# 192 channels held as 128 and twice 64, and delta rows twice: a change of layout in two linear stages of a vision kernel

## The chip, the cores and the metric

One Trainium2 chip, of which the program uses one core. The metric is device time in microseconds (us). The kernel before takes 18009.72 us, the median of 3 runs (18006.15 to 18019.03). Engines are named as in the profile: PE (TensorE, matmuls; PEld its weight loads), DVE (VectorE), ACT (ScalarE), POOL (GpSimd), SP (which issues the DMAs).

## What is computed

Two layers, one after the other, on 8 images of 64 x 64 tokens with 192 channels, all in float32.

Layer 0 (cut to what matters):

```python
xz = einsum('bhwc,dc->bhwd', x, W_in)            # 192 -> 2 x 384
xl, z = split(xz, 2)
xc = silu(depthwise3x3(xl) + conv_b)
y0, y1 = state_space_scan(xc), state_space_scan(transpose(xc))   # two directions
yg = (y0 + y1) * silu(z)
out = x + einsum('bhwd,cd->bhwc', yg, W_out)     # 384 -> 192
h1 = silu(einsum('...c,dc->...d', out, W1) + b1) # 192 -> 768
x1 = out + einsum('...d,cd->...c', h1, W2) + b2  # 768 -> 192
```

Layer 1 takes one half of the channels of x1 through three convolutions, the other half through a second state-space model with four scan directions:

```python
x_dbl = einsum('bkdl,kcd->bkcl', xs4, x_proj_w)  # dts (6 rows), Bs, Cs (16 rows each)
delta = softplus(einsum('bkrl,kdr->bkdl', dts, dt_proj_w) + dt_proj_b)
h = exp(delta * A) * h + (delta * u) * B         # step by step over 4096 tokens
y = sum_n(h * C)
```

then a norm, a gate and a projection, and adds x1.

## The kernel before, in words

Channels lie on the 128 partitions, tokens along the free dimension. The program is written out by hand: every instruction is pinned to program order, so each engine runs its instructions in the order in which the Python code emits them, and waits for data by semaphores.

**The scan** (`selective_scan`) is the frame. It works through 3072 units: 8 images x 8 steps of 1024 tokens (`LC`) x 3 tiles of channels x 16 units. A unit is 8 channels x 16 states on 128 partitions, 1024 tokens. Per unit: SP fetches `dA` (`fetch`, four units ahead), ACT makes the exponential (`decay`, L1322), PE spreads `dB` (`spread`, L1330, two small bf16 matmuls), DVE multiplies (`weigh`, L1345) and scans (`scan`, L1352), POOL multiplies by C (L1356), ACT carries the end on (`carry_on`, L1362, L1363). Every four units PE sums the states (`gather`, L1374, four 32-column matmuls beside each other, into `acc`). `project` (L1227) makes the rows of dt, B and C for a step; `prepare` (L1257 on) makes delta for the next tile: two matmuls `ps_dt` (L1262, twelve rows of dt, one for each half of 512 tokens, in two half units), ACT operations on each, and then softplus on ACT and POOL.

**Side work.** All else of an image is written as Python generators, and class `Beside` deals their pieces out between the scan's instructions. While image b is scanned, the side work is `conv0`, `ssd` and `mlp0` (layer 0) of image b + 1, `conv_branch` with `scan_sums` and `scan_outputs` of image b - 1, and `scan_inputs` and `transposed` of image b + 1. Each piece ends with a `yield` of its cost, a number that stands for PE time. `selective_scan` calls `beside.half()` twice per unit. Each call adds a rate to a credit and runs pieces until the credit is used up; a `yield None` ends the half at once. The rate is

```python
self.rate = (own + sum(self.costs.get(gen.__name__, 40.0) for gen in self.stages)) / halves
```

with `own` = 465.0 for the scan's own PE work, which is taken from the same credit by `beside.spend`, and `halves` = 768 (720 for the first and the last image). `beside.finish()` runs what is left at the seam between two images: 23 units before the next image's first unit, just ahead of the next image's loads of `u` and of its side work. The first image's layer 0, `scan_inputs` and `transposed` have no scan to run beside: they are the prologue, the first 990 us.

**PSUM.** `cx.one(name)` hands out a bank of 128 x 512 float32. Beside the scan four such banks rotate among all that calls it (`acc`, `ps_dt`, and all side work); the scan's `dB` has the other four. In the prologue eight rotate.

**What the change touches.** `mlp0` (L649) works on 256 tokens at a time, 16 times per image, as stages in turn (`load, add, gate, turn, project, expand, contract, store`). The 192 channels are two times 96 (`CH`): each of gate (L693, `ps_z`) and expand (L739, `ps_h`) takes two matmuls with 96 rows per 128 outputs, added up in PSUM; project (L726, `ps_o`) and contract (L757, `ps_m`) make two outputs of 96 columns. `conv0`'s `rows_in` (L362, `ps_in`) does the same as gate, on 512 tokens. ACT takes the results out with Silu (L697, L744) or as a copy (L365). Silu and Exp are in different tables of ACT, so a Silu between two `decay` operations brings table loads (ACT_TABLE_LOAD).

Of the kernel before, what the change touches and what calls it, by code (L numbers as in the profile page):

```python
# [41 lines left out]
NXP = 4 * NS + 2 * RK  # L42
# [66 lines left out]
def setup(cx, cp, dp, p0, p1):  # L109
# [42 lines left out]
    k["b2"] = const(p0["b2"].rearrange("(a p) -> p a", p=CH), [CH, 2], "b2")  # L152
# [34 lines left out]
    nc.sync.dma_start(out=k["dtw"][4 * NS : NXP], in_=p1["dtw"].rearrange("g r t m -> r g t m"))  # L187
# [138 lines left out]

def conv0(cx, x):
# [3 lines left out]
    with cx.pool("cw0") as wp, cx.pool("v0", 2) as vp:  # L331
        w_in = wp.tile([CH, 2, INNER0], F32, tag="w_in", name="w_in")
        pin(nc.sync.dma_start(out=w_in, in_=k["p0_w_in"].rearrange("(a p) m -> p a m", p=CH)[:, :, :INNER0]))
# [11 lines left out]
        first = vp.tile([CH, 2, R2 * WW], F32, tag="xt", name="first")[:, :, :WW]  # L345
        pin(nc.sync.dma_start(out=first, in_=x[:, 0:WW].rearrange("(a p) l -> p a l", p=CH)))
        xts, xcs = {}, {}

        def load(p):

            n = min(R2, HH - 1 - p * R2)
            xts[p] = vp.tile([CH, 2, R2 * WW], F32, tag="xt", name="xt")
            at = (p * R2 + 1) * WW
            pin(nc.sync.dma_start(
                out=xts[p][:, :, : n * WW], in_=x[:, at : at + n * WW].rearrange("(a p) l -> p a l", p=CH)
            ))

        def rows_in(j, src, n, at):

            ps = cx.one("ps_in")  # L360
            for a in range(2):
                pin(nc.tensor.matmul(  # L362
                    ps[:, : n * WW], lhsT=w_in[:, a, j * 128 : (j + 1) * 128], rhs=src[:, a, :], start=a == 0, stop=a == 1
                ))
            pin(nc.scalar.copy(  # L365
                pads[j][:, at : at + n, 1 : 1 + WW], ps[:, : n * WW].rearrange("p (h w) -> p h w", w=WW)
            ))

        def project(p, j):
            pad = pads[j]  # L370
            if p == 0:
                rows_in(j, first, 1, 1)
            else:
                pin(nc.gpsimd.tensor_copy(pad[:, 0:2, :], pad[:, R2 : R2 + 2, :]))
            for b in range(2):
                n = min(RB, HH - 1 - p * R2 - b * RB)
                if n < RB:
                    pin(nc.gpsimd.memset(pad[:, R2 + 1, :], 0.0))
                rows_in(j, xts[p][:, :, b * RB * WW : (b * RB + n) * WW], n, 2 + b * RB)
                yield 2.4  # L380
# [268 lines left out]
def mlp0(cx, x, x1):  # L649

    nc, pin, k = cx.nc, cx.pin, cx.k
    NF, T = HID // 128, 256
    with cx.pool("mw0") as wp, cx.pool("m0", 2) as mp:
        def weight(n, shape, src):
            t = wp.tile(shape, F32, tag=n, name=n)
            pin(nc.sync.dma_start(out=t, in_=src))
            return t

        w_z = weight("w_z", [CH, 2, INNER0], k["p0_w_in"].rearrange("(a p) m -> p a m", p=CH)[:, :, INNER0:])
        w_out = weight("w_out", [128, NJ, C], k["p0_w_out"].rearrange("(j p) m -> p j m", p=128))  # L660
        w1 = weight("w1", [CH, 2, HID], k["p0_w1"].rearrange("(a p) m -> p a m", p=CH))
        w2 = weight("w2", [128, NF, C], k["p0_w2"].rearrange("(f p) m -> p f m", p=128))
        gT = wp.tile([128, NJ, T], F32, tag="gT", name="gT")
        h1 = wp.tile([128, NF, T], F32, tag="h1", name="h1")
        tiles = (slice(0, 2), slice(2, 3))
        st = {}

        def cols(i):
            return slice(i * T, (i + 1) * T)

        def load(i):
            st[i] = {}
# [934 lines left out]
```

## Time and profile before

| | |
|---|---|
| median of 3 runs | 18009.72 us |
| profiled execution | 17986.38 us |
| its span (first to last instruction) | 17984.4 us |
| mean granted clock of TensorE | 0.815 of full speed |
| busy: PE, DVE, ACT, POOL | 80%, 68%, 60%, 67% |
| scan of h, DVE L1352 | 3072 x 2343 ns |
| weigh, DVE L1345 | 3072 x 1218 ns |
| matmuls of mlp0, PE L693, L726, L739, L757 | 437.2, 395.9, 749.3, 750.1 us busy |
| `ps_in`, PE L362 | 398.6 us busy |
| `ps_dt`, PE L1262 | 558.4 us busy |
| ACT_TABLE_LOAD | 1283 ns each |

Busy time is the union of a group's records: two matmuls that run at once count once, so the sum of count x mean can be above it. A float32 matmul appears as two records (two passes). A waiting engine is listed with the instruction that released it.

### The profile page before, as it was taken

To read this page: it belongs to the slowest core of one execution; us is meant where nothing else is said; L and a number is where in the kernel's file an instruction comes from. 1 tells how busy PE (TensorE), PEld (TensorE's weight loads), DVE (VectorE), ACT (ScalarE), POOL (GpSimd) and SP (SyncE) were. 2 spreads that over 40 slices of the span, in tenths; PEclk is the share of its full clock that TensorE was granted. 3 is DMA by queue.
4 is the path that set the end of the run, shared out by engine and by line. 5 is a ranking of instruction groups with operands and counts; after the bars stand their busy time and mean duration, and the time that the engine had idled before them with its cause. 6 is when DMAs were issued, how large, how long until landed. Compare 5 with 4: busy or idle time off the path is not lost. (4 is left out here: it accounts for less than half of the span.)

```text
span 17984.4 us, 224777 instructions
## 1 busy us (share of the span) xinstructions
PE 14375.7 (80%) x76904; PEld 5676.6 (32%) x76904; DVE 12309.3 (68%) x9392; ACT 10711.9 (60%) x18482; POOL 12008.5 (67%) x6437
## 2 busy tenths in 40 slices
PE   8977788788877888778878788787888778868776
PEld 4623332343223431334313342233422334211111
DVE  2167787776667766677657775677766777667785
ACT  2464676466664756647566485664756557555654
POOL 3168776776668755687657875678755786657774
PEclk9987788789787887878878798787987779877676
DMA  3277777777677776777767777777776777677785
GB/s 85 75 201 177 189 190 202 168 193 199 170 195 174 192 194 164 196 176 201 186 170 188 176 199 185 184 188 178 197 183 178 184 183 198 180 194 190 184 196 143
DMA packets 1600969, 3238.93 MB, mean 180 GB/s; under 512 B 391580, under 2 KB 869396, under 8 KB 1596244
## 3 DMA queue, kind: packets, MB, share of 16 engines
q1 hardware_dynamic: 1599828, 3224.55, 71.2%
q8 instruction: 614, 10.06, 0.3%
q14 instruction: 527, 4.32, 0.1%
HBM read 2545.63 MB, written 678.18 MB: 179 GB/s over the span
## 5 line engine op out<-in xcount | busy, mean ns | idle before, releaser
L1356 POOL TENSOR_TENSOR h<-h,bc 128x1023 f32<-128x1023 f32 x3072 | 7223.5, 2354 | 3926.6 <-DVE h L1352 3412.2
L1352 DVE TENSOR_TENSOR_SCAN h<-dA,carry,dB 128x1024 f32<-128x1024 f32 x3072 | 7198.8, 2343 | 624.0 <-ACT dA L1322 188.7
L1345 DVE TENSOR_TENSOR dB<-dB,bc 128x1024 f32<-128x1024 f32 x3072 | 3741.5, 1218 | 2996.7 <-PE dB L1330 2948.1
L1322 ACT ACTIVATE dA<-dA,neg_a 128x1024 f32<-128x1024 f32 x3072 | 3486.8, 1135 | 797.5 <-DMA dA<-dld 795.3
L1374 PE MATMUL acc<-h,gather 128*32 128x512 f32 x12288 | 2479.9, 758 | 525.7 <-POOL h L1356 203.2
L1378 ACT COPY y<-acc 128x512 f32<-128x512 f32 x1536 | 886.5, 577 | 1908.7 <-PE acc L1374 1891.4
L1330 PE MATMUL dB<-dus,spread 24*128 24x512 bf16 x6144 | 1418.8, 430 | 365.3 <-DVE h L1352 283.8
L795 PE MATMUL ps_c<-p,conv_w 96*96 96x512 f32 x2304 | 1250.9, 670 | 120.5 <-ACT p L816 105.8
L1330 PEld LDWEIGHTS <-spread 24*128 24x128 bf16 x6144 | 317.6, 93 | 2607.9 <-issue 1700.3
L620 PE MATMUL ps_y<-dtx,M 64*64 64x64 f32 x12288 | 824.3, 267 | 393.5 <-DVE Hn L611 387.1
L1363 ACT ACTIVATE h<-h,bc 128x1 f32<-128x1 f32 x3072 | 905.1, 295 | 163.3 <-ACT carry L1362 3.8
L620 PEld LDWEIGHTS ps_y<-dtx,M 64*64 64x64 f32 x12288 | 691.6, 177 | 572.8 <-issue 349.5
L1374 PEld LDWEIGHTS acc<-h,gather 128*32 128x32 f32 x12288 | 321.2, 119 | 1690.8 <-issue 836.4
L319 PE MATMUL ps_cv<-pad,diag 64*64 64x512 f32 x6912 | 849.9, 611 | 5.6 <-ACT xo L399 2.8
L1276 POOL TENSOR_TENSOR w<-w,e 128x1024 f32<-128x1024 f32 x192 | 452.6, 2357 | 510.7 <-ACT carry L1362 423.7
L757 PE MATMUL ps_m<-h,w 128*96 128x256 f32 x3072 | 750.1, 392 | 30.2 <-DVE gT L715 20.4
L739 PE MATMUL ps_h<-o,w 96*128 96x256 f32 x3072 | 749.3, 397 | 4.3 <-ACT zs L697 1.7
L1362 ACT COPY carry<-h 128x1 f32<-128x1 f32 x3072 | 575.4, 187 | 250.9 <-DVE h L1352 248.1
L739 PEld LDWEIGHTS ps_h<-o,w 96*128 96x128 f32 x3072 | 585.6, 196 | 174.6 <-issue 62.3
L795 PEld LDWEIGHTS ps_c<-p,conv_w 96*96 96x96 f32 x2304 | 367.5, 177 | 814.8 <-issue 703.3
L555 PE MATMUL ps_d<-R,after 128*128 128x384 f32 x1024 | 554.8, 631 | 84.6 <-DVE M L575 36.8
L106 ACT ACT_TABLE_LOAD x481 | 617.1, 1283 | 8.2
(244 smaller groups left out, 22124.1 us busy)
## 6 DMA issues: line engine op xcount, KB each, us to landing
dA<-dld SPq DMA_DIRECT2D x3072, 512.0 KB
dud<-terms SPq DMA_DIRECT2D x192, 768.0 KB
dus<-dud SPq DMA_DIRECT2D x2304, 64.0 KB
bc<-bcd SPq DMA_DIRECT2D x256, 512.0 KB
X<-xrows SPq DMA_DIRECT2D x1024, 96.0 KB
yrows<-yo SPq DMA_DIRECT2D x1024, 96.0 KB
y<-yrows SPq DMA_DIRECT2D x256, 384.0 KB
u<-u SPq DMA_DIRECT2D x192, 512.0 KB
```

The costliest lines, as they stand in the source:

```text
L319: pin(nc.tensor.matmul(ps[64 * b : 64 * (b + 1)].rearrange("p (h w) -> p h w", w=WW), lhsT=diag[:, t, :], rhs=pad[64 * i : 64 * (i + 1), b ...
L620: pin(nc.tensor.matmul(psy[d][here, h * HP : (h + 1) * HP], lhsT=M[here, d, h, :], rhs=dtx[here, d, h, :], start=True, stop=d == 1,))
L739: pin(nc.tensor.matmul(ps[:, n * T : (n + 1) * T], lhsT=w1[:, a, (f + n) * 128 : (f + n + 1) * 128], rhs=o[:, a, :], start=a == 0, stop=a ...
L795: pin(nc.tensor.matmul(ps.rearrange("p (h w) -> p h w", w=WW), lhsT=w[:, t, :], rhs=pad[:, dy : dy + RB, dx : dx + WW], start=t == 0, stop ...
L1322: pin(nc.scalar.activation(dAs[q], dAs[q], AF.Exp, scale=k["neg_a"][:, steps[m][1], t, i : i + 1]))
L1330: pin(nc.tensor.matmul(dBs[q][:, half, :], lhsT=k["spread"][at : at + 3 * UD, :], rhs=du_of[n][at : at + 3 * UD, i // 2, :], start=True, s ...
L1345: pin(nc.vector.tensor_mul(dBs[q], dBs[q], of(q)[0]))
L1352: pin(nc.vector.tensor_tensor_scan(order(h, g), order(dA, g), order(dB, g), carry, ALU.mult, ALU.add))
L1356: pin(nc.gpsimd.tensor_mul(h[:, rest], h[:, rest], C_[:, rest]))
L1363: pin(nc.scalar.activation(end, end, AF.Identity, scale=C_[:, last : last + 1]))
L1374: pin(nc.tensor.matmul(ps[32 * v : 32 * (v + 1)], lhsT=k["gather"], rhs=hs[q - 3 + v][:, here], start=True, stop=True))
L1378: pin(nc.scalar.copy(y[:, here], ps))
```

## The change

- `mlp0` and `conv0` hold the 192 channels as a tile of 128 channels and a tile of 64 channels in which two blocks of tokens lie below each other (partitions 0 to 63 and 64 to 127). `load_split` loads weights so (the 64-row part twice), and `product` makes the result of two blocks: two matmuls with 128 rows, then two with 64 rows, one in each half of the rows of PE. Where 192 channels are the output, `narrow` makes 128 columns for both blocks in one matmul of 512 tokens, and then 64 columns for each block, one in each half of the columns of PE.
- `mlp0` thus takes 512 tokens at a time, 8 times per image, with an order of its own in place of `in_turn`: gate(i), expand(i-1), turn(i), contract(i-1), project(i). Silu(z) is written into `gT`, and `turn` multiplies there in place. The costs in its yields are new, and so are those in `conv0`.
- The rows of dt are made twice in `project` (rows 64 to 75 and 96 to 107, by doubled weight columns), so `prepare` issues the two `ps_dt` matmuls one behind the other on different rows of PE. Both banks are taken at once; the ACT operations on them stay in the half units in which they were. `own` becomes 450.0.

The diff, cut to its core (`load`, `first` and the setup of `b2` follow the same layout):

```diff
-NXP = 4 * NS + 2 * RK
+DTS = (64, 96)
+NXP = DTS[1] + 2 * RK
...
-    nc.sync.dma_start(out=k["dtw"][4 * NS : NXP], in_=p1["dtw"].rearrange("g r t m -> r g t m"))
+    for at in DTS:
+        nc.sync.dma_start(out=k["dtw"][at : at + 2 * RK], in_=p1["dtw"].rearrange("g r t m -> r g t m"))
...
+def load_split(cx, pool, tag, src, m):
+    a, b = (pool.tile([128, m], F32, tag=tag + v, name=tag + v) for v in "ab")
+    cx.pin(cx.nc.sync.dma_start(out=a, in_=src[0:128]))
+    for i in range(2):
+        cx.pin(cx.nc.sync.dma_start(out=b[64 * i : 64 * (i + 1)], in_=src[128:C]))
+    return a, b
+def product(cx, outs, weight, cols, xa, xbs):
+    nc, pin = cx.nc, cx.pin
+    for out, x in zip(outs, xa):
+        pin(nc.tensor.matmul(out, lhsT=weight[0][:, cols], rhs=x, start=True, stop=False))
+    for b, (out, x) in enumerate(zip(outs, xbs)):
+        pin(nc.tensor.matmul(out, lhsT=weight[1][64 * b : 64 * (b + 1), cols], rhs=x, start=False, stop=True))
...
-        w_in = wp.tile([CH, 2, INNER0], F32, tag="w_in", name="w_in")
-        pin(nc.sync.dma_start(out=w_in, in_=k["p0_w_in"].rearrange("(a p) m -> p a m", p=CH)[:, :, :INNER0]))
+        w_in = load_split(cx, wp, "w_in", k["p0_w_in"][:, :INNER0], INNER0)
...
         def project(p, j):
             pad = pads[j]
+            cols = slice(j * 128, (j + 1) * 128)
             if p == 0:
-                rows_in(j, first, 1, 1)
+                ps = cx.one("ps_in")
+                product(cx, [ps[:, :WW]], w_in, cols, [first[0]], [first[1]])
+                rows_in(j, ps, 1, 1)
             else:
                 pin(nc.gpsimd.tensor_copy(pad[:, 0:2, :], pad[:, R2 : R2 + 2, :]))
-            for b in range(2):
-                n = min(RB, HH - 1 - p * R2 - b * RB)
-                if n < RB:
-                    pin(nc.gpsimd.memset(pad[:, R2 + 1, :], 0.0))
-                rows_in(j, xts[p][:, :, b * RB * WW : (b * RB + n) * WW], n, 2 + b * RB)
-                yield 2.4
+            ns = blocks(p)
+            if ns[1] < RB:
+                pin(nc.gpsimd.memset(pad[:, R2 + 1, :], 0.0))
+            pss = [cx.one("ps_in") for b in range(2)]
+            xa, xb = xts[p]
+            product(
+                cx, [ps[:, : n * WW] for ps, n in zip(pss, ns)], w_in, cols,
+                [xa[:, b * RB * WW : (b * RB + n) * WW] for b, n in enumerate(ns)],
+                [xb[64 * b : 64 * (b + 1), : n * WW] for b, n in enumerate(ns)],
+            )
+            yield 1.8
+            for b, n in enumerate(ns):
+                rows_in(j, pss[b], n, 2 + b * RB)
+            yield 1.8
...
+        gT = wp.tile([128, 2, NJ, T], F32, tag="gT", name="gT")
+        h1 = wp.tile([128, NF, 2, T], F32, tag="h1", name="h1")
...
+        def load_x(i):
+            a = mp.tile([128, 2 * T], F32, tag="xa", name="xa")
+            pin(nc.sync.dma_start(out=a, in_=x[0:128, i * 2 * T : (i + 1) * 2 * T]))
+            b = mp.tile([128, T], F32, tag="xb", name="xb")
+            for v, low in enumerate(lows):
+                pin(nc.sync.dma_start(out=b[low], in_=x[128:C, (2 * i + v) * T : (2 * i + v + 1) * T]))
+            xs[i] = a, b
...
+        def gate(i):
+            for js in tiles:
+                pss = [cx.one("ps_z") for b in range(2)]
+                n = js.stop - js.start
+                for j in range(n):
+                    at = slice(j * T, (j + 1) * T)
+                    cols = slice((js.start + j) * 128, (js.start + j + 1) * 128)
+                    product(cx, [ps[:, at] for ps in pss], w_z, cols, *both(*xs[i]))
+                    if j + 1 < n:
+                        yield 1.8
+                for b, ps in enumerate(pss):
+                    pin(nc.scalar.activation(
+                        gT[:, b, js, :].rearrange("p j t -> p (j t)"), ps[:, : n * T], AF.Silu
+                    ))
+                yield 1.8
+            cx.exp_again()
+        def turn(i):
+            for b, (y, _) in enumerate(ys.pop(i)):
+                pss = []
+                for js in tiles:
+                    ps = cx.one("ps_t")
+                    for j in range(js.start, js.stop):
+                        for q in range(2):
+                            at = (j - js.start) * T + q * 128
+                            pin(nc.tensor.transpose(ps[:, at : at + 128], y[:, q, j * 128 : (j + 1) * 128], k["ident"]))
+                    pss.append(ps)
+                yield 1.2
+                yield None
+                for js, ps in zip(tiles, pss):
+                    g = gT[:, b, js, :].rearrange("p j t -> p (j t)")
+                    pin(nc.vector.tensor_mul(g, ps[:, : (js.stop - js.start) * T], g))
+        def narrow(weight, n, rhs, psa, psb):
+            for f in range(n):
+                pin(nc.tensor.matmul(psa, lhsT=weight[:, f, 0:128], rhs=rhs(f), start=f == 0, stop=f == n - 1))
+                yield 1.2
+            for f in range(n):
+                for b, low in enumerate(lows):
+                    pin(nc.tensor.matmul(
+                        psb[low, :T], lhsT=weight[:, f, 128:C], rhs=rhs(f)[:, b, :], start=f == 0, stop=f == n - 1
+                    ))
+                yield 0.6
+        def project(i):
+            xa, xb = xs.pop(i)
+            oa = mp.tile([128, 2 * T], F32, tag="oa", name="oa")
+            ob = mp.tile([128, T], F32, tag="ob", name="ob")
+            psa, psb = (cx.one("ps_o") for v in range(2))
+            yield from narrow(w_out, NJ, lambda j: gT[:, :, j, :], psa.rearrange("p (b t) -> p b t", b=2), psb)
+            yield None
+            pin(nc.vector.tensor_add(oa, psa, xa))
+            pin(nc.vector.tensor_add(ob, psb[:, :T], xb))
+            os[i] = oa, ob
+        def expand(i):
+            for f in range(0, NF, 2):
+                pss = [cx.one("ps_h") for b in range(2)]
+                for n in range(2):
+                    at = slice(n * T, (n + 1) * T)
+                    cols = slice((f + n) * 128, (f + n + 1) * 128)
+                    product(cx, [ps[:, at] for ps in pss], w1, cols, *both(*os[i]))
+                    if n == 0:
+                        yield 1.8
+                for n in range(2):
+                    for b, ps in enumerate(pss):
+                        pin(nc.scalar.activation(
+                            h1[:, f + n, b, :], ps[:, n * T : (n + 1) * T], AF.Silu, bias=k["b1"][:, f + n : f + n + 1]
...
+                yield 1.8
+        def contract(i):
+            oa, ob = os.pop(i)
+            psa, psb = (cx.one("ps_m") for v in range(2))
+            yield from narrow(w2, NF, lambda f: h1[:, f, :, :], psa.rearrange("p (b t) -> p b t", b=2), psb)
+            yield None
+            pin(nc.vector.scalar_tensor_tensor(oa, psa, k["b2"][:, 0:1], oa, ALU.add, ALU.add))
+            pin(nc.vector.scalar_tensor_tensor(ob, psb[:, :T], k["b2"][:, 1:2], ob, ALU.add, ALU.add))
+            yield 0.6
+            yield None
+            pin(nc.sync.dma_start(out=x1[0:128, i * 2 * T : (i + 1) * 2 * T], in_=oa))
+            for v, low in enumerate(lows):
+                pin(nc.sync.dma_start(out=x1[128:C, (2 * i + v) * T : (2 * i + v + 1) * T], in_=ob[low]))
+        load_x(0)
+        load_y(0)
+        for i in range(NI + 1):
+            if i < NI:
+                yield from gate(i)
+                add(i)
+            if i > 0:
+                yield from expand(i - 1)
+            if i < NI:
+                yield from turn(i)
+                if i + 1 < NI:
+                    load_x(i + 1)
+                    load_y(i + 1)
+            if i > 0:
+                yield from contract(i - 1)
+            if i < NI:
+                yield from project(i)
...
-            for i, here in enumerate(halves):
-                ps = cx.one("ps_dt")
-                pin(nc.tensor.matmul(
-                    ps, lhsT=k["dtw"][4 * NS : NXP, g, t, :], rhs=rows[4 * NS : NXP, here], start=True, stop=True
-                ))
-                beside.spend(1.2)
+            pss = [cx.one("ps_dt") for here in halves]
+            for ps, at, here in zip(pss, DTS, halves):
+                took = slice(at, at + 2 * RK)
+                pin(nc.tensor.matmul(ps, lhsT=k["dtw"][took, g, t, :], rhs=rows[took, here], start=True, stop=True))
+            beside.spend(1.2)
+            for i, (ps, here) in enumerate(zip(pss, halves)):
                 yield 1 + i
...
-        beside.spread_over(halves, 465.0)
+        beside.spread_over(halves, 450.0)
...
-                (4 * NS + RK * e, w[:RK]),
+                *((at + RK * e, w[:RK]) for at in DTS),
```

## The prediction

> **What bounds the kernel now.** I read the page first: busy times, then the chain that ended last.
>
> ```profile
> PE 14375.7 (80%) x76904; PEld 5676.6 (32%) x76904; DVE 12309.3 (68%) x9392; ACT 10711.9 (60%) x18482; POOL 12008.5 (67%) x6437
> ...
> PE 14%; DMA 10%; ACT 7%; POOL 6%; DVE 6%; issue 3%; SPq 1%; DVEq 0%; POOLq 0%; ACTq 0%
> ```
>
> No engine is full and the chain hops between all of them; PE (TensorE) has most in both. The view of waits says what the scan stands for:
>
> ```profile
> POOL h L1356 <- DVE h L1352: 3412.2, 1383, 24.4
> DVE dB L1345 <- PE dB L1330: 2948.1, 959, 111.3
> ```
>
> POOL only follows DVE. DVE needs 2.343 + 1.218 = 3.56 us per unit (3072 units), and its great wait is for `dB`, a small matmul queued on PE behind side work. So PE time counts where it holds `dB` up. Busy times by stretch: the prologue's MLP, then MLP, conv branch and scan_outputs beside the scan of image 3.
>
> ```profile
> core 0: us, PE busy (x) PEld busy (x) DVE busy (x) ACT busy (x) POOL busy (x), PEclk, DMA share, GB/s
> 524.00:790.00 266.00, 257.26 (x1215) 207.63 (x1214) 40.61 (x81) 129.52 (x187) 28.74 (x18) 0.98 0.21 64
> ...
> 8153.00:8675.00 522.00, 451.14 (x1920) 248.07 (x1924) 400.79 (x288) 412.38 (x656) 370.64 (x168) 0.89 0.76 195
> 8675.00:9005.00 330.00, 283.67 (x768) 77.96 (x760) 191.26 (x108) 153.67 (x279) 187.96 (x97) 0.89 0.73 192
> ```
>
> The prologue's MLP is PE alone. The MLP beside the scan takes 522 us for 104 units, 5.0 us each: PE 4.34, DVE 3.85, ACT 3.97 per unit. The last view is the timeline at the seam between two images (7178 on; the last line is the first seam):
>
> ```profile
> 7189.23 14.62 ACT L994 COPY part<-whole 128x1024 f32<-128x1024 f32 x8 [10.69 <-issue]
> ...
> 7220.95 1.09 PE L362 MATMUL ps_in<-first,w_in 96*128 96x64 f32 x4 [42.14 <-DMA y<-y]
> 7230.53 1.23 DVE L1345 TENSOR_TENSOR dB<-dB,bc 128x1024 f32<-128x1024 f32 x1 [48.95 <-PE dB L1330]
> ...
> 2834.37 1.23 DVE L1345 TENSOR_TENSOR dB<-dB,bc 128x1024 f32<-128x1024 f32 x1 [23.91 <-PE dB L1330]
> ```
>
> At 7180 the next image's side work is added, but what is left of this one's must be issued first, in one piece: some of `scan_inputs` and all of `transposed`. PE stands 42 us at the next conv0's first matmul, since SP issues that load only after `transposed`'s copies and stores. At the first seam `transposed` had been spread in time: 24 us.
>
> **What the skill says.** TensorEngine Tiling (Array Packing), Key Properties: a change of tiling mode drains TensorE. TensorE: Matmul & The Clock Gate, The mechanism (Part 3): matmuls on different row or column groups run together. The PE timeline agrees with both:
>
> ```profile
> 603.33 5.35 PE L757 MATMUL ps_m<-h,w 128*96 128x256 f32 x24
> 608.51 3.83 PE L739 MATMUL ps_h<-o,w 96*128 96x256 f32 x17
> ...
> 149.04 1.70 PE L408 MATMUL ps_p<-xp,xc 64*128 64x140 f32 x24
> 150.67 5.81 PE L319 MATMUL ps_cv<-pad,diag 64*64 64x512 f32 x52
> ...
> 7176.43 1.06 PE L1374 MATMUL acc<-h,gather 128*32 128x512 f32 x8
> 7177.43 0.39 PE L1330 MATMUL dB<-dus,spread 24*128 24x512 bf16 x2
> ```
>
> A matmul of f32 shows as two passes. 24 passes of 256 columns take 5.18 us: 0.216 each, 0.84 ns a column. The 24 half-height passes of 140 columns would take 2.83 one by one; they took 1.63: pairs (1.42) and a switch (0.2). `acc`'s eight passes, four at a time, are 2 x 0.43 = 0.86, and `dB`, in another mode, starts after 1.00: a switch of 0.14. I take 0.16. The same page's Part 1 has the clock fall when PE idles; here 0.98 in the prologue and 0.89 beside the scan. PSUM — Partial Sum Buffer, Specifications: 8 banks. Beside the scan four rotate in `one`, the others hold `dB`.
>
> **The change, part by part.** *MLP matmuls*, per 512 tokens. Before, 72 matmuls = 144 passes x 0.216 = 31.1 us. After, nine products of 4 full and 2 paired passes, and `narrow` with 3 and 6 steps of two long passes (4 short) and two paired ones: 54 + 18 + 36 = 108 pass times, 23.3 us; but each product enters and leaves the 64-row mode (18 switches), each `narrow` the 64-column mode (4): 22 x 0.16 = 3.5. Net 26.8, 4.3 saved, 34 us an image; gate and expand gain almost nothing (1.62 for 1.73 per product). *conv0*: twelve products of 512 columns: 3.46 - 2.59 - 0.32, 7 us an image. *dt*: the groups show 558.4 us busy for 384 matmuls, 1.45 each; two go as one, so 24 tiles x 1.45 = 35 us an image. The twelve rows sit in row groups of their own, in `dB`'s mode.
>
> *ACT*: Silus come in fours, not twos; in program order table loads fall from 1197 to 1000, 197 x 1.283 us / 8 = 32 us an image. DVE: the same counts, hidden. DMA: the same bytes; 16 more issues of some 0.5 us for x and x1 an image and 8 in conv0, hidden because `dA` is fetched four units ahead; without that cover 12 us. The store comes half a unit after its add, so `dA` fetches behind it on SP can wait; same cover. Wider `rows` copies cost nothing (partitions).
>
> *The spreading.* Each half unit gives side work rate = (own + costs)/768. Summing yields: mlp0 347.2 to 283.2, conv0 251.2 to 236.8, own 465 to 450, so 2.230 becomes 2.109. Stepping the credit through the yields, conv0, ssd, mlp0, branch, outputs, scan_inputs took 154, 183, 207, 108, 50, 66 halves with 13 of cost and `transposed` left over; now 151, 181, 179, 111, 51, 84, and `transposed` fills the last 11. So MLP loses 14 units, and the seam loses its bulk work.
>
> *MLP beside the scan.* PE after: 451 - 34/0.89 - 9 (dt) - 19 (14.5 units' own matmuls, 1.31 each) = 389 for 89.5 units, 4.34 as before. ACT: 412 - 32 - 36 = 344, 3.84. So 5.0 us a unit again. Against it stands a wait the trace doesn't show: banks now go in pairs, and the third pair waits for the first pair's four Silus. Bound: 0 (PE waits for ACT are 12 us in that window) to 1 us per pair, nine pairs per 512 tokens, 0.8 us a unit. I take 0.1: the copies have a product of 3 us to hide in. 89.5 x 5.1 = 456 for 520: -64 an image.
>
> *The rest of an image.* scan_inputs, `transposed` and seam: before 178 (33 units) + 65 (2) = 243. In image 0, which was spread so already, 51 units took 245, 4.80 each; 47.5 x 4.80 = 228, and a seam of 33 as the first: +18. Other stages: 31 us of PE saved there (dt 25, conv0 6), and I count 12, as waits of other kinds end there too. Sum -58. For images 1 to 5 -290, with 20 back for image 1, whose MLP took 500; image 6's seam was short (39): -32. Together -302. Image 0: MLP -60, `scan_inputs` with `transposed` +12, 9.5 units of scan alone at 4.4 +42, 2.5 more units of conv0 and ssd +9, dt -10: -7. Image 7: dt alone, -12. Prologue (eight banks, PE full): -34, conv0 -5. Sum -360: span 17984 to 17624; the median shown, 18009.7, is 25 above that execution's span: **17650**.
>
> **The rivals.** *Pair waits decide* (slower). Place: `product` in mlp0 beside the scan, four banks, the ACT queue ahead of the Silus. For it: at 8303 ACT stood 7.1 us for a late `dA` and PE then waited 3.5 for a bank with single ones already. Against: 12 us in 522. It turns the sign at 360/8 = 45 us an image, 0.6 us per pair; at 1 us, 8 x (72 - 45) slower: 18220. *Halves do not overlap*: the switches are added and nothing is saved, PE at 5.0 and the MLP at 5.7 us a unit: 54 us an image, dt's 12 and the prologue's 67 on top: 18200. `ps_p` speaks against. *DMA holds the MLP*: its bytes (102 MB) lose only 14.5 units' dA; 90 MB at 190 instead of 198 GB/s is 20 us an image: 17790. For it: 195 GB/s now; against: conv0's stretch runs at 205. *PE converts fully*: MLP at 4.8 a unit (-27) and the others at two thirds (-10), seven images: 17390.
>
> **How the numbers follow.** Likeliest 0.47 (its own range 17500 to 17830), full conversion 0.17, DMA 0.20, pair waits 0.10, no overlap 0.03, else 0.03. Time 17650; the range 17370 to 17920 leaves out the slower rival, no overlap and the fast end of full conversion. 0.2% (36 us) is about what a measurement of this kernel can tell from no change. Faster: 0.47 + 0.17 + 0.20 = 0.84; pair waits between 0.6 and 0.7 us leave 0.05 within; slower 0.11.
>
> **What would show it.** MLP stretches near 456 us; `ps_h`'s paired passes starting together; DVE's wait at the seams near 24 us, not 49; wait of PE for ACT in the MLP below 40 us an image; the prologue's MLP near 230 us; dt's PE time halved; 250 us less of ACT tables. The prediction is wrong if PE waits for Silus at every third pair, or if switches cost over 0.3 us.

## The result, and the profile after

The changed kernel takes 17895.4 us (median of 4 runs, 17849.8 to 17937.8), the kernel before 18014.4 us beside it (4 runs): a ratio of 0.9936 (95% interval 0.9914 to 0.9959). The sign was right and the time lies in the range, but only 119 us came where 360 were forecast. The profiled execution took 17849.8 us, span 17848.0.

From the page of the changed kernel, the busy times and the chain that ended last:

```profile
PE 13899.7 (78%) x75752; PEld 4872.4 (27%) x75752; DVE 12241.7 (69%) x9264; ACT 10450.0 (59%) x18285; POOL 12006.8 (67%) x6437
...
PE 13%; DMA 10%; ACT 8%; DVE 6%; POOL 5%; issue 4%; SPq 1%; DVEq 0%; POOLq 0%; ACTq 0%
```

PE has 476 us less to do, ACT 262 us less. The span fell by 136. The chain is as mixed as it was. The view of waits, the same two lines as before:

```profile
POOL h L1426 <- DVE h L1422: 3474.7, 1393, 22.4
DVE dB L1415 <- PE dB L1400: 3067.7, 879, 108.6
```

At this pace DVE waits longer for `dB` (3068 us, before 2948), although PE's work fell: PE comes later with less to do. The stretches, with the columns of the prediction's table: the prologue's MLP, then MLP and conv branch beside the scan of image 3.

```profile
500.00:737.00 237.00, 228.99 (x1078) 125.17 (x1079) 33.19 (x62) 92.52 (x160) 28.91 (x16) 0.97 0.27 84
...
8113.00:8582.00 469.00, 380.76 (x1684) 162.21 (x1685) 342.62 (x242) 353.15 (x579) 320.70 (x147) 0.87 0.75 194
8582.00:8923.00 341.00, 282.78 (x778) 77.58 (x777) 197.93 (x112) 156.34 (x283) 194.03 (x100) 0.91 0.74 193
```

Where PE is alone, the prologue, its gain arrives whole: 237 us for 266. Beside the scan the MLP takes 469 us for 89 units, 5.27 each, where it took 522 for 104, 5.0 each. PE's busy time per unit fell from 4.34 to 4.28, so more of each unit is PE standing, and the granted clock of the stretch is 0.87 for 0.89. The timeline (start, duration, instruction, idle time before it): a product of the MLP with `dB` behind it and the start of a later one, then the seam at 7157 and the first seam.

```profile
8310.53 1.13 PE L350 MATMUL ps_h<-oa,w1a 128*128 128x256 f32 x4
8311.59 0.70 PE L352 MATMUL ps_h<-ob,w1b 64*128 64x256 f32 x4
8312.23 0.39 PE L1400 MATMUL dB<-dus,spread 24*128 24x512 bf16 x2
...
8316.81 1.13 PE L350 MATMUL ps_h<-oa,w1a 128*128 128x256 f32 x4 [0.46 <-ACT h L807]
...
7171.32 0.66 PE L350 MATMUL ps_in<-first,w_ina 128*128 128x64 f32 x2 [17.98 <-DMA xa<-in_x_dram]
7182.65 1.23 DVE L1415 TENSOR_TENSOR dB<-dB,bc 128x1024 f32<-128x1024 f32 x1 [33.96 <-PE dB L1400]
...
2840.74 1.23 DVE L1415 TENSOR_TENSOR dB<-dB,bc 128x1024 f32<-128x1024 f32 x1 [23.45 <-PE dB L1400]
```

The paired passes do overlap: four of them end 0.70 us after they start, and the next matmul starts 0.64 us after they did, where four passes of 0.216 one by one would be 0.86. The seam is shorter: DVE waits 34 us where it waited 49, the first seam is as it was.

Where the 136 us of the two profiled executions came from, read off the scan's records from seam to seam: prologue -36, image 0 +44, image 1 +8, images 2 to 6 -35, -12, -4, -2 and -8, image 7 -90. (The border is the scan of the 23rd unit before the next image, so the seam ahead of image 7, shorter by some 29 us, is in its -90.) Images 1 to 6, where 302 us were expected, gave 53. Their stages, as means over images 2 to 6; a stage is taken here from its first matmul to the next stage's first, so its borders are a few us off those of the prediction, which followed the credit:

| | before, us | after, us |
|---|---|---|
| seam | 53 | 25 |
| conv0 | 373 | 378 |
| ssd | 571 | 565 |
| mlp0 | 509 (104 units, 4.89 each) | 460 (89 units, 5.17 each) |
| conv branch | 337 | 344 |
| scan_outputs | 164 | 164 |
| scan_inputs, transposed | 180 | 237 |
| sum | 2186 | 2174 |
| PE busy in it | 1767 | 1707 |

PE lost 60 us of work an image and the image 12 us. 48 us more of idle PE stand between them.

### The profile page after: what moved, and what is told of

Read it like the earlier page. It is cut to its first block, busy times and chain, and to the rows that moved or that the text cites. A ratio compares the mean times of both kernels' runs of the same rounds, so it can differ in the third digit from the quotient of the medians.

```text
span 17848.0 us, 222371 instructions
## 1 busy us (share of the span) xinstructions
PE 13899.7 (78%) x75752; PEld 4872.4 (27%) x75752; DVE 12241.7 (69%) x9264; ACT 10450.0 (59%) x18285; POOL 12006.8 (67%) x6437
## 5 line engine op out<-in xcount | busy, mean ns | idle before, releaser
L1400 PE MATMUL dB<-dus,spread 24*128 24x512 bf16 x6144 | 1368.2, 433 | 464.7 <-DVE h L1422 368.4
L661 PE MATMUL ps_y<-dtx,M 64*64 64x64 f32 x12288 | 750.9, 251 | 359.0 <-DVE Hn L652 355.7
L661 PEld LDWEIGHTS ps_y<-dtx,M 64*64 64x64 f32 x12288 | 630.3, 162 | 561.9 <-issue 357.2
L596 PE MATMUL ps_d<-R,after 128*128 128x384 f32 x1024 | 594.9, 672 | 95.2 <-DVE M L616 57.3
L350 PE MATMUL ps_h<-oa,w1a 128*128 128x256 f32 x1536 | 495.8, 449 | 160.7 <-ACT h L807 94.2
L598 ACT ACTIVATE M<-ps_d 128x384 f32<-128x384 f32 x512 | 247.2, 488 | 443.0 <-PE ps_d L597 442.5
L776 PE MATMUL ps_m<-h,w 128*128 128x512 f32 x768 | 417.2, 683 | 96.4 <-ACT h L807 54.5
L1297 PE MATMUL ps_xp<-u,xp 128*108 128x512 f32 x768 | 442.2, 663 | 57.2 <-DMA u<-u 36.6
```

The source lines that it names most:

```text
L661: pin(nc.tensor.matmul(psy[d][here, h * HP : (h + 1) * HP], lhsT=M[here, d, h, :], rhs=dtx[here, d, h, :], start=True, stop=d == 1,))
L1400: pin(nc.tensor.matmul(dBs[q][:, half, :], lhsT=k["spread"][at : at + 3 * UD, :], rhs=du_of[n][at : at + 3 * UD, i // 2, :], start=True, s ...
```

## The experiments

Ratios are to the kernel before on the same chip, where its median was 17986 to 17998 us. Where nothing else is said, all of a kernel computes what the changed one does.

### One part alone, or one part taken back

`dt_only`: the kernel before with dt's part.

```diff
-NXP = 4 * NS + 2 * RK
+DTS = (64, 96)
+NXP = DTS[1] + 2 * RK
...
+            pss = [cx.one("ps_dt") for here in halves]
+            for ps, at, here in zip(pss, DTS, halves):
...
-        beside.spread_over(halves, 465.0)
+        beside.spread_over(halves, 450.0)
...
-            po = vp.tile([128, 2, 2 * NP0], F32, tag="po", name="po")
+            po = vp.tile([128, 2, 2 * NP0], F32, tag="po", name="po", bufs=1)
```

> The kernel before with the dt part of the change alone (dt rows and weights twice, both halves of a row together, 450 for 465), MLP and input projection as before; conv0's tile po has one buffer instead of two, for room. The prediction counted 12 us an image for it, 8 x 12 = 96: 17918. If the last image's 90 us of the changed kernel are dt's alone (its MLP and conv0 are not beside that image), the same in all eight would be some 500: 17500. If PE's time for dt is hidden everywhere: within 36 us of 18014. Theory A of the lost gain (pair waits eat what MLP and conv0 save) needs a value near the changed kernel's 17895, between 17850 and 17950.

Measured: 17852.2 us, ratio 0.9918 (0.9895 to 0.9941). dt's part alone gives as much as the whole change. That is more than the 96 us counted, and it leaves nothing over for MLP and conv0, less than nothing once the prologue's 36 us are taken off. The single buffer of `po` is a change of its own: ACT waits 172 us in all for `po`'s stores here, and not at all in the changed kernel. What that costs was not measured by itself.

`mlp0_old`: the changed kernel with the MLP of before (function `mlp0` and the constant `b2` swapped back, nothing else).

> The changed kernel with the MLP (mlp0) of before: conv0's and dt's parts stay. Theory A (pair waits in both stages take about what the new matmuls save there): MLP's own effect beside the scan is small, so only the prologue's gain of some 31 us and a little more go: 17925 to 17950. The prediction's step (MLP saves 64 us in each image from 1 to 7, less what other stages pay for the lost units): 17895 + 31 + 7 x 40 = 18200. Theory C (the MLP's pair waits cost more than its matmuls save): faster than 17860.

Measured: 17950.1 us, ratio 0.9973 (0.9962 to 0.9984). Theory A's numbers are 0.995 to 0.9964 of 18014; the measured one lies just past their far end, and its interval reaches them. Beside `dt_only` it is 0.55% slower, so conv0's part looked dear.

`conv0_old`: the changed kernel with the conv0 of before (function `conv0` swapped back, `po` with one buffer).

> The changed kernel with the input projection (conv0) of before; dt's part and the MLP's stay; conv0's tile po has one buffer instead of two, for room. dt's part alone gave a ratio of 0.9918, and dt's with conv0's part 0.9973. Theory A (conv0's part costs, by pairs of banks held over a pause in conv0): without it 0.55% comes back: ratio 0.988 to 0.990, some 17800. Theory B (any part beside dt's only shifts the stages, and what it costs is not its own): 0.992 to 0.995, as dt's part alone and as the whole change.

Measured: 18042.9 us, ratio 1.0024 (1.0014 to 1.0034). Both theories missed. Without conv0's part the kernel is 0.9% slower, with it (and without the MLP's) 0.55% slower. A part cannot cost in one pairing and gain in the other by its own work; `ps_in`'s busy time fell by the same 50 us in both kernels that have the new conv0 (420.6 before; 373.8 and 370.7). The single `po` (131.8 us of ACT's waits here) could be part of it, but `dt_only` has it too and is fast. Something that all these kernels share seemed to move the time.

`first_only`: `dt_only`, with the changed MLP in the prologue.

```diff
-            beside.add(mlp0(cx, x[b], x1[b]))
+            beside.add((mlp0_first if b == 0 else mlp0)(cx, x[b], x1[b]))
...
-        beside.costs.update(conv_branch=190.0, scan_outputs=78.0)
+        beside.costs.update(conv_branch=190.0, scan_outputs=78.0, mlp0=347.2)
```

> The kernel before with dt's part (as in the run of dt's part alone) and the changed MLP in the prologue alone, where no scan runs beside it; the MLP of images 1 to 7 and conv0 are those of before. If the MLP's matmuls save what they do in the changed kernel's prologue (34 us) and cost nothing there later: ratio 0.9918 - 0.0019 = 0.990, some 17805. If the MLP's saving beside the scan is real and only the spreading hid it: slower than 0.990 by nothing that shows; then the changed kernel with another pace would be the better one.

Measured: 17780.3 us, ratio 0.9888 (0.9869 to 0.9907). That is the sum of dt's part and the prologue's gain, and the fastest kernel of this study. Where no scan runs beside it, the MLP's new form is worth what its matmuls save.

### Is dt's gain the overlap?

`dt_same_rows`, in the changed kernel:

```diff
-DTS = (64, 96)
+DTS = (64, 64)
```

> The changed kernel with one number changed: both halves' dt matmuls read the rows from 64 on (DTS 64, 64), so that they are issued together as in the changed kernel but use the same rows of TensorE. Theory A (dt's gain is the overlap of its halves): dt's busy time goes from 331 us back to some 560, and the time by what dt's part gave, 0.8%: ratio 1.000 to 1.003. Theory D (the gain is the order: one wait, one change of mode and one interruption instead of two): busy time goes up but the ratio stays at 0.992 to 0.996.

Measured: 18033.1 us, ratio 1.0025 (1.0013 to 1.0036), theory A. The groups of PE by shape (count | busy us, mean ns | idle before), first of the changed kernel, then of this one:

```profile
L1333 PE MATMUL ps_dt<-rows,dtw 12*128 12x512 f32 x768 | 331.1, 845 | 84.0 <-ACT u L1033 16.5 <-ACT xc L428 12.0 <-ACT bc L590 11.7
```

```profile
L1333 PE MATMUL ps_dt<-rows,dtw 12*128 12x512 f32 x768 | 531.9, 822 | 92.4 <-ACT xc L428 15.5 <-ACT u L1033 12.9 <-ACT bc L590 11.6
```

201 us more of PE time, and some 0.9% (160 us) more of time. Program order, banks and pace are those of the changed kernel, so nothing is dealt out differently: in this kernel and at this pace the overlap of the two halves is what gains, at some 0.8 us of time for each us of PE. Other paces were not tried.

### Waits for banks taken in pairs

`conv0_soon`: conv0's copies straight after their product, the pause after them.

```diff
-            yield 1.8
             for b, n in enumerate(ns):
                 rows_in(j, pss[b], n, 2 + b * RB)
-            yield 1.8
+            yield 3.6
```

> The changed kernel, but conv0 issues the copies of both banks (rows_in) straight after their product, and the pause of 1.8 between product and copies comes after them (3.6 in all). In the changed kernel PE waits some 57 us for ACT in image 3's conv0, some 30 in the kernel before. Theory A (the pause holds two of the four banks over a half unit and makes PE wait): these waits fall to 30 us or less, conv0 goes from 376 us to 350 to 360, and 7 images give 100 to 180 us: 17715 to 17795. Theory B (the waits are ACT's own lateness, behind the scan's work, and return elsewhere): within 36 us of 17895.

Measured: 17885.6 us, ratio 0.9945 (0.9930 to 0.9960); conv0 takes 379 us an image as before the edit (378), and PE's waits for ACT in it stayed at 50 to 57 us an image. Theory B: the pause in conv0 held nothing up.

`soon_both`: in addition, expand's Silus come after each product, two by two.

```diff
                     product(cx, [ps[:, at] for ps in pss], w1, cols, *both(*os[i]))
-                    if n == 0:
-                        yield 1.8
-                for n in range(2):
                     for b, ps in enumerate(pss):
                         pin(nc.scalar.activation(
...
+                    if n == 0:
+                        yield 1.8
```

> The changed kernel, but expand issues the two Silus of a product straight after it instead of four after two products, and conv0 its copies straight after their product. Theory A (pair waits hold the MLP): PE's waits for ACT's h and gT in image 3's MLP fall from some 40 us to 20 or less, the MLP beside the scan from 5.2 us a unit to 4.95, and 7 images give some 140 us: ratio 0.986. Theory C (PE has less work, so it is idle more, runs at a lower granted clock and is late as often: the waits for ACT are where it idles, not why): waits may fall, the time stays within 0.2% of 0.994.

Measured: 18346.8 us, ratio 1.0198 (1.0177 to 1.0218), far off both. From the view of PE's waits (us in total, times, longest), the changed kernel and then this one:

```profile
PE ps_h L350 <- ACT h L807: 94.2, 36, 7.3
PE ps_m L776 <- ACT h L807: 54.5, 7, 7.8
PE ps_t L765 <- ACT h L807: 51.3, 24, 3.0
PE ps_h L350 <- ACT gT L750: 42.4, 25, 3.0
```

```profile
PE ps_h L350 <- ACT h L803: 581.8, 192, 11.2
PE ps_h L350 <- ACT gT L749: 42.0, 25, 4.2
```

The second product writes to the bank that the first one's Silus read, so now it waits for them, 192 times. The edit meant to shorten a wait made one. It shows what such waits cost all the same: `conv0_soon` has 280 us of PE's waits for the MLP's Silus, this kernel 645, and 2.5% more time (some 455 us) goes with these 365 us. It holds 84 table loads more than the changed kernel too, 108 us of ACT, so not all of the 455 is the wait.

`no_pause`: expand issues both products and their four Silus in one go.

```diff
-                    if n == 0:
-                        yield 1.8
...
-                yield 1.8
+                yield 3.6
```

> The changed kernel, but expand issues both products of a pair of banks and their four Silus in one go, and the pause between the products comes after them (3.6 in all): the pair is held for about half a unit less. With the Silus split up, each product waited for the Silus of the product before in its bank: 488 us more of PE's waits for ACT's h, and 450 us more of time. Theory A (the pair waits hold the MLP): PE's waits for ACT's h in the MLP fall from 33 to some 15 us an image, and 0.92 of that comes off the time, 7 x 18 x 0.92 = 115 us: ratio 0.987 to 0.989. Theory E (larger pieces of side work delay dB, so what is saved in one wait comes back in the other): waits fall, ratio 0.993 to 0.998.

Measured: 17937.9 us, ratio 0.9965 (0.9950 to 0.9981), theory E's number. Its waits:

```profile
PE acc L1442 <- ACT h L805: 65.4, 27, 5.7
PE ps_t L765 <- ACT h L805: 58.3, 33, 3.0
PE ps_h L350 <- ACT h L805: 40.5, 21, 3.0
```

`ps_h` waits less (40 for 94), but `acc`, the scan's own matmul, which waited 25 us for these Silus in the changed kernel, now waits 65. Whoever next needs one of the four banks waits; moving a pause changes who. In all the waits fell from 282 to 232 us, DVE's wait for `dB` grew from 3068 to 3104, and the time did not fall. So theory E's account fits too, though these 36 us are few.

### The pace

`seam_only`: the kernel before with `spread_over(halves, 525.0)` for 465.0, so that nothing is left over for the seam.

> The kernel before with one number changed: spread_over takes 525 instead of 465, so that scan_inputs and transposed are spread over the last units of an image and nothing is issued in bulk at the seam. Theory A (the prediction's: the bulk work at the seam costs 24 us more than the first seam does, and the same work costs less when spread): DVE's wait for dB at the seams falls from some 45 us to some 24, and the sum is 15 us an image better, 7 images: 18014 - 100 = 17910. Theory B (side work costs as much spread as in bulk, since the units that take it up get longer by about what the seam loses): the seam's wait falls all the same, and the time is within 36 us of 18014.

Measured: 18023.4 us, ratio 1.0019 (1.0008 to 1.0029), theory B. The seam shrinks from 53 to 13 us an image, scan_inputs with transposed grows from 180 to 266. An image takes 2188 us for 2186. The bulk work at the seam was no loss to be won back.

The next four vary the pace alone. `after_440` and `after_460`: the changed kernel with 440.0 and 460.0 for 450.0; `first_440`: the same edit to `first_only`.

> The changed kernel with its pace alone changed: 440 for 450 in spread_over, so that all side work stands up to a few units later against the scan. It computes the same with the same instructions. Theory S (where the stages stand against the scan's own work moves the time by some 0.5%, so the parts' effects found so far, of 0.5 to 1%, hold such shifts): differs from 0.9936 to 0.9945 by more than 0.3%. Theory P (the pace is smooth): within 0.15%.

> The changed kernel with its pace alone changed: 460 for 450 in spread_over. Theory S: differs from 0.9936 to 0.9945 by more than 0.3%, in either direction. Theory P: within 0.15%, a little slower, as 525 was against 465 in the kernel before (0.19%).

> The version with dt's part and the changed MLP in the prologue alone (ratio 0.9888), with 440 for 450. Theory S: differs from 0.9888 by more than 0.3%, in either direction. Theory P: within 0.15%.

Measured: 18160.3 us, 1.0090 (1.0074 to 1.0105); 17867.9 us, 0.9933 (0.9917 to 0.9948); 18009.6 us, 1.0012 (1.0002 to 1.0022). Theory S, and more than it asked for: ten parts in 450 make the changed kernel 1.5% slower and the other 1.2%. In `after_440` the MLP costs 5.38 us a unit, ssd 586 us for 565, and transposed falls back into the seam (45 us).

`first_460`, `after_475`, `conv0_old_465`, `before_480`, and then `before_450` and `first_455`: the number in `spread_over` alone, as the names say.

> The version with dt's part and the changed MLP in the prologue alone, with 460 for 450 in spread_over. With 450 it has a ratio of 0.9888, with 440 1.0012. If only the drop at 440 is a step (at the seam, where transposed falls back into one piece), 460 stays at 0.987 to 0.990; if the pace scatters the time anywhere, it differs by more than 0.3%.

> The changed kernel with 475 for 450 in spread_over. 450 gave 0.9936 and 460 0.9933. If above the step at 440 the pace is flat: 0.992 to 0.995. If the changed kernel's lost gain is the pace's, some pace gives clearly less: under 0.990. By the prediction's sum it should have given 0.980.

> The kernel with dt's and the MLP's parts and the conv0 of before, with 465 for 450 in spread_over; with 450 it has a ratio of 1.0024 and its seams last 42 us, as those of the changed kernel do at 440. Theory 2 (the pace): at 465 it comes down to the changed kernel's 0.992 to 0.995, and conv0's part had no effect of its own of 0.9%. Theory 1 (the parts' own effects): it stays above 1.000.

> The kernel before with 480 for 465 in spread_over. 525 gave 1.0019. If the kernel before stands on a good pace already, 0.999 to 1.005; if it also has a step (its seams hold bulk work still), a higher pace takes it away and gives 0.988 to 0.995: then dt's gain of 0.8%, measured at another pace, would be in part the pace's.

> The kernel before with the pace of the change alone: 450 for 465 in spread_over. If the kernel before is flat in its pace (1.0000, 0.9993, 1.0019 at 465, 480, 525): 0.998 to 1.003, and the number 450 did nothing by itself. If it scatters as the kernels with dt's part do: off by more than 0.3% in either direction.

> The version with dt's part and the changed MLP in the prologue alone, with 455: 450 gave 0.9888, 460 gave 1.0000. If the time moves smoothly between them: 0.993 to 0.996. If 450 is a single good point: 0.998 to 1.002; if the good stretch goes on to 455: 0.987 to 0.991.

All ratios by pace:

| pace | 440 | 450 | 455 | 460 | 465 | 475 | 480 | 525 |
|---|---|---|---|---|---|---|---|---|
| before | | 1.0042 | | | 1 | | 0.9993 | 1.0019 |
| dt's part, MLP in the prologue | 1.0012 | 0.9888 | 0.9920 | 1.0000 | | | | |
| whole change | 1.0090 | 0.9936 | | 0.9933 | | 1.0001 | | |
| dt's and MLP's parts | | 1.0024 | | | 1.0054 | | | |

Intervals are 0.0008 to 0.0019 to each side (0.0023 for the whole change at 450). `first_455` lies between its neighbours, so 450 lies in a narrow dip and is not a single lucky point. No pace of the four brings the changed kernel under 0.990. `conv0_old_465` did not come down, so theory 2 does not account for that kernel. `before_450` shows that the change's number by itself costs 0.4% in the old kernel, and `before_480` that the pace next to it gives nothing. Since dt's pair takes 1.2 from the credit once and not twice, 24 times an image, `dt_only` at 450 leaves the side work what the kernel before has at 479; the two then hold their stages within one unit of each other. Between them (0.9918 and 0.9993) dt's part is worth 0.75%, near the 0.9% of `dt_same_rows`. Both are numbers for pace 450. At 440 and 460 the kernel with dt's part and the MLP in the prologue takes 1.0012 and 1.0000, no less than the kernel before at 465 or 480, so dt's gain is not shown at those paces.

Where the pace's time goes can be read from DVE's waits for `dB` (us in total, times, longest): the changed kernel at 460 and 440, then the other at 450 and 440.

```profile
DVE dB L1415 <- PE dB L1400: 2866.6, 932, 108.5
...
DVE dB L1415 <- PE dB L1400: 3339.1, 909, 109.2
...
DVE dB L1535 <- PE dB L1520: 2773.9, 887, 109.1
...
DVE dB L1535 <- PE dB L1520: 3118.5, 891, 109.0
```

At a slow pace `dB` comes late: the other kernel's waits are 2774, 2850, 3015 and 3119 us at 450, 455, 460 and 440, in the order of its times, and the changed kernel's longest, too, is at 440. But this is one execution each, and the wait does not account for the time alone: at 450 and 460 the changed kernel takes the same time with 3068 and 2867 us of it, and the kernel before has its shortest, 2793, at 525, where it is not fastest.

### What holds at every pace

Between its best and its worst pace the kernel before differs by 0.5%, the other two by 1.2% and 1.6%; so much of a time can be the pace's. What is the same at all paces is the MLP's price beside the scan. Means over images 2 to 6, stages from first matmul to first matmul, units counted from the scan's records:

| | us a unit in mlp0 | an image, us |
|---|---|---|
| old MLP beside the scan: ten kernels | 4.82 to 4.97 | 2172 to 2196 |
| new MLP, Silus in fours: nine kernels | 5.15 to 5.41 | 2171 to 2217 |
| `soon_both` | 5.82 | 2232 |

The ranges of the price do not touch, those of the image overlap. The new MLP gives up 14 units and makes the others dearer, and the units that it gives up cost some 5 us wherever they go. The stretch of image 3's MLP in five kernels, with the columns of the prediction's table: the kernel before, `dt_only`, the changed one, `conv0_old` and `soon_both`.

```profile
8169.00:8681.00 512.00, 447.27 (x1913) 244.15 (x1914) 399.45 (x288) 409.38 (x655) 363.65 (x165) 0.90 0.76 195
```

```profile
8130.00:8621.00 491.00, 424.07 (x1896) 236.72 (x1894) 392.23 (x282) 405.95 (x650) 357.20 (x162) 0.92 0.79 204
```

```profile
8127.00:8592.00 465.00, 381.01 (x1680) 159.06 (x1678) 345.44 (x243) 350.89 (x577) 318.11 (x145) 0.88 0.74 191
```

```profile
8215.00:8688.00 473.00, 380.65 (x1660) 158.61 (x1663) 341.18 (x240) 336.18 (x558) 308.14 (x141) 0.86 0.73 189
```

```profile
8333.00:8854.00 521.00, 398.13 (x1677) 165.79 (x1673) 343.47 (x242) 366.49 (x584) 317.68 (x145) 0.83 0.65 170
```

PE stands 65 and 67 us in the first two, 84, 92 and 123 in the others, and its clock, 0.90 and 0.92 in the first two, is 0.88, 0.86 and 0.83 in the others. DVE's busy time falls only because fewer units lie in the stretch.

## Why the prediction was right and wrong

In short: the work was counted rightly, and the step from PE's work to time failed. A unit of the MLP was to cost 5.0 us again, since PE has as much to do in it, and 0.1 for waits; over images 2 to 6 its price rose by 0.28. And three other stages, in which 12 us an image were to be saved, took 7 more.

**Right: what the work costs.** The groups of the MLP's matmuls (gate, project, expand, contract) fall from 2332.5 to 2088.0 us busy, 31 us an image for 34 counted. Gate and expand together gave 11 us in all, "almost nothing" as said: in the prologue a product starts every 1.69 us, before every 1.73. conv0's gave 6 an image for 7, dt's 28 for 35. (These are sums of groups, which overlap a little.) Table loads went from 1197 to 1000, as counted, and the wider `rows` copies take 580 ns for 577. The prologue gave 36 us for 39. That the halves do not overlap is ruled out by `ps_dt` and by the timeline.

**Right: the order of the side work.** The stages take the units that the credit said (89 for the MLP), and the seam lost its bulk. It stayed at 34 us of DVE's wait for 24, since conv0's first loads come later than at the first seam: PE stood 18 us for `xa`, where it had stood 11 for `first`.

**Wrong: the MLP at 5.1 us a unit.** The step "I take 0.1" was mis-sized. PE's waits for the Silus of gate and expand, over all PE instructions, went from 86 to 282 us: 196 us in seven images, 28 an image, 0.31 a unit. The largest of them before, to set beside those of the changed kernel above:

```profile
PE ps_dt L1262 <- ACT h L744: 17.4, 7, 4.1
PE acc L1374 <- ACT h L744: 16.7, 19, 3.2
PE ps_t L709 <- ACT h L744: 16.3, 11, 3.3
```

The price went up by nearly as much: over images 2 to 6 from 4.89 to 5.17 us a unit (the prediction's 5.0 came from one stretch that was dearer than this mean). The "nine pairs" per 512 tokens were a miscount: there are nine products, and `gate` and `expand` take five pairs of banks for them, so the wait is 0.39 us a product, 0.70 us a pair. The prediction's mark, less than 40 us of PE's waits for ACT in an image's MLP, was missed: 29 to 33 us before, 54 to 61 after (all of ACT; the 12 us it read before are about the Silus' share). It took a product of 3 us to cover the copies. But the Silus stand in ACT's queue among the scan's exponentials, and where the two follow each other a table load of 1283 ns lies between them; the changed kernel has 1000 table loads. The Trainium skill has it in Trainium Kernel Development and Optimization, Best Practices: "TensorE tiling speeds up compute but not PSUM evacuation"; these waits agree. But the wait is not the whole price: `conv0_old` has 212 us of these waits and the dearest MLP of the nine, 5.41, and `no_pause` has 50 us less than the changed kernel and is no faster. What sets the rest is not shown.

**Wrong: "PE 4.34 as before".** The sum given, 451 - 34/0.89 - 9 - 19, is 385 and not 389, which makes 4.30 a unit; measured were 4.28. So PE's work was right, and yet a unit took longer: PE's busy time alone did not set it. This is the step that failed furthest: that a unit costs 5.0 us again because PE has as much to do in it, in a stage where PE's share was 87% and its next instruction often waits for ACT or DVE. At this pace 60 us off PE's work brought 12 us off an image, and MLP and conv0, with half of the 60, brought none that can be told: their PE work turned into idle PE.

**Wrong: the rest of an image, -12 and +18.** From scan_outputs to the seam it was +30, and conv0, ssd and conv branch, where 12 us were to be saved, took 7 more. These are 31 of the 46 us that an image gained less than forecast (12 for 58); the MLP, -49 for -64, is the other 15. `seam_only` shows the first without the change: side work that is spread costs the units what the seam gains, so 4.80 us a unit, taken from the first image, was too low; some 5.1 was measured in the changed kernel. The seven I cannot put to a cause; ssd alone, untouched, takes between 564 and 586 us in the kernels shown.

**Wrong: images 0 and 7.** -7 became +44 and -12 became -90. As much comes from pace alone: with the same borders the kernel before at 525 shows +51 and -82, at 480 +29 and -41.

**Rivals.** Full conversion is out. The slower one, pair waits, was to turn the sign at 45 us an image; 28 came. It names a part of what was lost in the MLP. That DMA holds the MLP came nearest in time (17790), yet its mark is missing: `dt_only` moved 204 GB/s in this stage and the changed kernel 191, which speaks against a ceiling at 190.

**What stays open.** Why 2% of pace makes 1.5% of time. The stages' places against the scan's half units move (`after_440`: MLP, ssd and seam all dearer) and DVE waits longer for `dB`, but what on PE makes `dB` late was not isolated. So the change's 0.64% is a number for this pace. At 460 it is the same; at 475 it is nothing, and at 440 a loss of 0.9%. dt's overlap (0.75 to 0.9%) is shown at 450 alone. The prologue's 36 us (0.2%) are read from a stretch in which no scan runs, so no pace bears on them. MLP and conv0 beside the scan come to +0.5% at 450, +0.8% at 440 and -0.7% at 460, against the version without them: no gain that can be told from none, where the prediction counted 360 - 39 - 96 = 225 us, 1.2%.

## What to carry to other kernels

Before PE's saved time is counted as saved time, look at what PE waits for in that stage: where it already stands 13% of the stage, in a ring in which PE, ACT and DVE wait for each other, saved matmuls can become idle PE, and with banks taken in pairs PE waited longer for the copies. A saving where PE is alone (prologue) came through, and at the pace of the change one in the scan's own queue (dt). And where side work is dealt out by a pace, run each variant at three paces or more before its time is read as its own.

## What the runs showed of the hardware

- A change between full and 64-row passes cost 0.20 us, not the 0.16 taken: in the prologue a product starts every 1.69 us where six passes of 0.216 are 1.30, and has two changes.

```profile
526.17 1.13 PE L350 MATMUL ps_h<-oa,w1a 128*128 128x256 f32 x4
527.23 0.70 PE L352 MATMUL ps_h<-ob,w1b 64*128 64x256 f32 x4
527.86 1.13 PE L350 MATMUL ps_h<-oa,w1a 128*128 128x256 f32 x4
```

- Less work for PE went with a slower clock. In the profiled executions the mean granted clock is 0.812 to 0.820 in all ten kernels with the old MLP beside the scan, 0.804 to 0.809 in the nine with the new one and 0.797 in `soon_both`; in the MLP's stretches of images 2 to 6 it was 0.91 before and 0.88 after, while PE's share fell from 87% to 82%. The Trainium skill, TensorE: Matmul & The Clock Gate, Part 1, has the clock follow how busy PE was, and the runs agree in direction, so part of the saving may have been given back as slower matmuls. Whether and how much was not measured by itself.
